# A recurrence's product on VectorE instead of GpSimd, with new rules for the list that orders the engines: a two-layer attention and LSTM kernel on one core

## The chip, the core and the metric

The kernel runs on one core of one Trainium2 chip. The metric is the device time of one execution in microseconds, the median of the runs of a measurement. TensorE (PE in the profile; PEld are its weight loads), VectorE (DVE), ScalarE (ACT), GpSimd (POOL) and SyncE (SP, whose queue issues the DMAs) each work through their own instructions in order and wait for each other by semaphores.

## The reference

Everything is float32. The input `x` is 8 images of 56 x 56 positions with 256 channels. Cut to what matters:

```python
# layer 0: attention between regions of 8 x 8 positions, 49 regions, 8 heads
x = x + conv_attn(group_norm(x))        # each region: its 4 best regions by pooled q.k; 256 keys;
                                        # softmax over the 32 largest of the 256 scores; depthwise 3x3 on v
# layer 1, on t = x as 8 x 3136 tokens
t = t + window_attn(layer_norm(t))      # 7 neighbours
t = t + lstm(layer_norm(t))

def step(carry, xs):                    # 3136 steps, one after the other, 8 images at once, 256 wide
    h, c = carry
    i_t = sigmoid(xi_t + h @ V_i); f_t = sigmoid(xf_t + h @ V_f)   # f_t is computed, but not used
    g_t = tanh(xg_t + h @ V_c);    o_t = sigmoid(xo_t + h @ V_o)
    c_new = h * c + i_t * g_t           # the product h*c of this document
    h_new = o_t * tanh(c_new)
    return (h_new, c_new), h_new
```

The output has the shape of `x`.

## The kernel before

**Two kinds of work.** The recurrence (`recurrence`, one block of 16 tokens, `step(t)` for each token) is one chain of 3136 steps. All the rest, called background here, is layer 0 and the window attention: 56 units of one row of regions of one image (`units`), each with 7 calls of `region`, and the stages `queries_and_lepe`, `project` and `window_attention` of the neighbouring units spread between them. The first row of all images must be through before token 3 can start; the recurrence of one row of regions then goes beside the background of the next; and the last row of tokens (from `APART` = 2685 on) has no background left beside it.

**One step.** `sums_of` adds h times the gates' weights to the input terms that `place_terms` has put into the PSUM bank `r_sum` (24 matmuls of 64 columns, 48 instructions in the trace). ScalarE takes the tanh (`r_th`). VectorE transposes it in blocks of 32 x 32 into the gates' places of a buffer `r_cell`, of which there are two, for even and odd steps. One VectorE scan (`r_c`) then makes the new cell state: `r_cell` holds the gates and, in every third element of one part, the product h*c of the step before. ScalarE takes tanh of half of it (`r_tc`), and VectorE makes h (`r_hs`, from the output gate and that tanh). From token 2685 on, the output gate has sums, a tanh and a transpose of its own (`r_th2`, `r_tr2`).

The product h*c in the version before: ScalarE halves the cell state right after `r_tc` (`r_half`), GpSimd multiplies it with h into the other `r_cell` (line 308 like all of them, since a recorder makes every instruction), and a no-operation of VectorE (`seen_by`) waits for GpSimd's semaphore before the scan of the next step reads it.

**VectorE's background.** A region's 4 x 4 rounds of top-8 (`top`, MAX8) and replacement (`left`, MATCH_REPLACE8) on 128 x 256 scores are most of it. GpSimd's long operations are the subtraction `pe` - `left` (128 x 256) for each of 1568 score tiles, and additions of the same width on `gs`, `v`, `x` and `sum`.

**The list.** `_Plan` records every operation with a duration: `held`, the time it keeps its engine, and `late`, the time to its result, from `_time` or from `nc.timed` and `nc.together`. `run` then goes through time by these durations and takes for each free engine the first ready operation by rank (the chain's first), as long as it would not delay the next chain operation of its engine beyond a slack. What it takes, in that order, is the program's order on each engine; the semaphores follow from the data. `HOP` is the time from one engine to another, `SLACK` and, for VectorE, 1.5 times the time left, say how late an operation may make the chain. Operations with two SBUF operands (`op.pair`) are never listed on VectorE and GpSimd at the same time (`locked`), and long ones of GpSimd must start within three chain operations after h. Where TensorE would be idle for more than `FILL` = 220 ns, the list puts in a matmul whose result nobody reads (`fill`, tile `spare`).

Of the kernel before, what the change touches and what calls it, by code (L numbers as in the profile page):

```python
# [19 lines left out]
P = 128  # L20
# [20 lines left out]
TB = 16  # L41
XB = 8
# [15 lines left out]
HOP = 70  # L58
FAR = 10**12
FILL = 220  # L60
LONG = 400
CLEAR = 250
# [41 lines left out]
def _time(engine, name, view, reads, args, kw):  # L104

    n = max([_count(v) for v in [view] + reads])
    if engine == "SP":
        return 650, 2400 + 9 * n // 4
    if engine == "PE":
        held = 160 if name == "transpose" else 5 * _count(view) // 3 + 50  # L110
        return held, held + 140
    if engine == "POOL":
        t = 180 + 15 * n // 7
        return (1050, 1050) if ALU.pow in args else (t, t)
    if engine == "ACT":
        if kw.get("accum_out") is not None:
            t = 5 * n // 7 + 195
            return t + 90, t + 180
        t = n + 10
        if view.buf.banks:  # L120
            return t + 70, t + 120
        if not any(v.buf.banks for v in reads):
            t += 50
        if isinstance(kw.get("bias"), _View):
            return t + 80, t + 170
        return t, t + 90
    held = 25 * n // 24 + 60
    if name == "reciprocal":
        return 20 * n // 3 + 60, 20 * n // 3 + 150
    if name == "transpose":  # L130
        return held + 40, held + 120
    if name == "tensor_tensor_scan":
        return 2 * n + 80, 2 * n + 170
    if name == "match_replace":
        return held + 65, held + 150
    if name == "scalar_tensor_tensor":
        return held + 20, held + 100
    return held, held + 90
# [72 lines left out]
class _Op:  # L211
    __slots__ = (
        "engine", "trace", "held", "late", "rank", "chain", "before", "open", "due", "start",
        "takes", "pair", "made", "closes", "behind",
# [25 lines left out]
class _Plan:  # L240
# [79 lines left out]
    def seen_by(self, engine, op, view):  # L320


        def trace():
            made = engine.engine.engine_nop()
            self.tc.add_manual_dep(
                made.ins, op.made[0].ins.name,
                mybir.DependencyInfo(mybir.DependencyClass.Sync, mybir.DependencyReason.DATA),
                reason="seen before it is read",
            )

        self.add(engine.name, [trace], [view], [], 10, 10)
        return self.ops[-1]

    def add(self, engine, traces, reads, writes, held, late):
        op = _Op()
        op.engine, op.trace, op.held, op.late = engine, traces, held, late
        op.rank, op.chain = self.mode
        op.rank = (op.rank, len(self.ops))
        op.before, op.takes, op.start = {}, [], None
        op.closes, op.behind = False, None  # L340
        op.pair = engine in ("DVE", "POOL") and sum(
            not v.buf.banks and _count(v) > 8 for v in reads
        ) > 1
        self.ops.append(op)
        for views, write in ((reads, False), (writes, True)):
            for v in views:
                self._depend(op, v, write)
                if v.buf.pool is not None:
                    if not v.buf.users:
                        op.takes.append(v.buf)  # L350
                    if not v.buf.users or v.buf.users[-1] is not op:
                        v.buf.users.append(op)
# [19 lines left out]
    def _edge(self, a, b, whole):  # L372

        gap = a.late + HOP if a.engine != b.engine else a.late + 30 if whole else a.held
        a.before[b] = max(gap, a.before.get(b, 0))


    def run(self, tc, fill):
# [52 lines left out]
        filled = tied = 0  # L431
        locked = {"DVE": 0, "POOL": 0}
        since, closed = 0, None
        while len(done) < len(ops) + filled:
            moved = False
            for e in engines:
# [8 lines left out]
                until = due + (SLACK[e] if e != 'DVE' else max(20, 1.5 * (due - now)))  # L445
                for i, (rank, op) in enumerate(ready[e]):
                    if not op.chain and now + op.held > until:
                        continue
# [9 lines left out]
                    op.start = now  # L458
                    free[e] = now + op.held
# [4 lines left out]
                    heappush(events, now + op.late + HOP)  # L464
# [4 lines left out]
                    for b, gap in op.before.items():  # L469
                        b.due = max(b.due, now + gap)  # L470
                        b.open -= 1
                        if not b.open:
                            opened(b)
                    if op.chain:
                        at += 1
                        since += 1
                        if op.closes:
                            since, closed = 0, op
                    elif e == "POOL" and op.rank[0] == 0:
                        tied += 1  # L480
                    moved = True
                    break
            if not moved and free["PE"] <= now:

                due = min([expected("PE")] + [op[0] for op in later["PE"][:1]])
                if FILL < due - now < FAR // 2:
                    op = _Op()
                    op.trace, op.start = [fill], now
                    filled += 1
                    done.append(op)  # L490
                    free["PE"] = now + FILL
                    heappush(events, free["PE"])
                    moved = True
# [6 lines left out]
        self.length = now  # L500
        with tc.manual_schedule():
            for op in done:
                for t in op.trace:
                    t()

# [24 lines left out]
def _layers(ctx: ExitStack, tc, a, out):  # L530
# [129 lines left out]
    def fill():  # L660
        raw.tensor.matmul(  # L661
            spare[:32, :P], ident[:, :32], ident, start=True, stop=True, skip_group_check=True
# [15 lines left out]
    state = {"seen": None, "h": hss[1][:, :, TB - 1].as_of(hss[1][:, :, TB - 1, LAST:])}  # L678
# [135 lines left out]
    def queries_and_lepe(b, unit, im, row):  # L814
# [81 lines left out]
        def convolve(m):  # L896
            pl = bank()
            for dx in range(3):
                with nc.together(100 * L, 100 * L + 200):
# [22 lines left out]
    def region(qi, unit, im, row):  # L922
# [35 lines left out]
        for pair in range(groups // 2):  # L958
            both = ps_sc.tile([P, 2, 512], F32, name="sc")
            with nc.rank(0.5), nc.together(540, 740):  # L960
# [52 lines left out]
        for k in range(2):  # L1013
            with nc.together(280, 480):
# [11 lines left out]
        with nc.together(350, 550):  # L1026
# [310 lines left out]

    def recurrence(blk):
# [12 lines left out]
        def step(t):  # L1351
# [5 lines left out]
            cell, after = cells[at % 2], cells[(at + 1) % 2]  # L1357
# [5 lines left out]
            if at < APART:  # L1363
                with nc.rank(0, chain=True):
                    sums_of(bank_of(at)[:, now], h, (0, 1, 2), (680, 855))
# [3 lines left out]
                    nc.vector.transpose(gates, blocks(th))  # L1369
            else:  # L1370
# [19 lines left out]
            with nc.rank(0, chain=True):  # L1390
# [11 lines left out]
                if state["seen"]:  # L1402
                    nc._edge(state["seen"], nc.ops[-2], False)
# [5 lines left out]
            half = rwork.tile([P, 2, nb], F32, name="r_half")  # L1409
            nc.scalar.activation(half, c[:, :, :, 2], AF.Copy, scale=0.5)  # L1410
            hc = after[:, CELL + 2 : 2 * CELL + 2].rearrange("p (k b e) -> p k b e", b=nb, e=3)
            nc.gpsimd.tensor_tensor(hc[:, :, :, 2], hn, half, ALU.mult)
            with nc.rank(-1):
                state["seen"] = nc.seen_by(nc.vector, nc.ops[-1], hc[:, :, :, 2])
# [82 lines left out]
    for s in after(len(units) - 1):  # L1497
        s()
    made["tokens"] = SHIFTED
# [70 lines left out]
```

## Time and profile before

| | |
|---|---|
| three runs | 9196.0, 9199.82, 9213.82 us; median 9199.82 |
| the profiled execution | 9180.4 us, span 9178.5 us, granted TensorE clock 0.993 |
| first h of the recurrence starts at | 1340.4 us |
| last h starts at | 9173.2 us |
| busy: PE, DVE, ACT, POOL | 8792.1, 7559.4, 5939.4, 3221.5 us |
| of PE, the fill matmuls on `spare` | 14904 instructions, 2072.2 us |
| instructions | 500794 |

A busy time is the time in which the engine has at least one instruction under way. A duration is from an instruction's start to its end; on VectorE and TensorE the next one can start before that end. Almost all instructions have line 308 in common, where the recorder calls the engine, so they are told apart by their tiles (`out<-in`).

### The profile page before, as it was taken

The numbers are of one execution on the slowest core, as the hardware profiler recorded it, in microseconds if no ns is written. First come the engines' busy times: TensorE is split into PE (matmuls) and PEld (weight loads), VectorE is DVE, ScalarE is ACT, GpSimd is POOL, SyncE is SP. The second block draws the span as 40 slices with busy tenths as digits, with TensorE's granted clock in tenths as the row PEclk, the third lists the DMA queues.
The fourth block names the chain that finished last, engine by engine and source line by source line (L and its number), as shares of the span: only waits on it lengthen the run. The fifth ranks groups of instructions, "written<-read, shape, count | busy, mean of one in ns | idle before, by whom it ended". The sixth has DMA issues, their size and how long they took to land.

```text
span 9178.5 us, 500794 instructions
## 1 busy us (share of the span) xinstructions
PE 8792.1 (96%) x203918; PEld 6037.0 (66%) x203918; DVE 7559.4 (82%) x32392; ACT 5939.4 (65%) x23551; POOL 3221.5 (35%) x7747
## 2 busy tenths in 40 slices
PE   7999999999999999999999999999999999999999
PEld 4555556666666666666666666666666666688888
DVE  5776799999999899999899999899999999734443
ACT  4665667776666677676676676677766766534444
POOL 1232344444343343343344443434434444311111
PEclk9999999999999999999999999999999999999999
DMA  6545433333332333333333333233333232210000
GB/s 198 155 129 163 111 106 82 93 92 80 93 91 78 91 84 90 89 85 91 88 82 92 91 82 90 78 93 88 83 92 89 80 90 78 60 28 23 23 24 21
DMA packets 1071271, 798.40 MB, mean 87 GB/s; under 512 B 402366, under 2 KB 1001524, under 8 KB 1068964
## 3 DMA queue, kind: packets, MB, share of 16 engines
q1 hardware_dynamic: 1068964, 766.36, 30.8%
q8 instruction: 1604, 26.28, 1.2%
q14 instruction: 703, 5.76, 0.2%
HBM read 527.08 MB, written 238.88 MB: 83 GB/s over the span
## 4 chain that ended last, share of the span: by engine, by line
PE 52%; DVE 25%; ACT 6%; issue 2%; DMA 1%; SPq 0%; POOL 0%; ACTq 0%; DVEq 0%; POOLq 0%
PE r_sum L308 19%; PE mm L308 15%; PE spare L661 12%; DVE left L308 8%; DVE top L308 6%; DVE r_c L308 3%; PE pt_av L308 3%; PE sc L308 3%; DVE r_cell L308 2%; DVE r_hs L308 2%; ACT pe L308 1%; ACT r_th L308 1%; ACT xln L308 1%; DVE st L308 1%; ACT r_sum L308 1%
## 5 line engine op out<-in xcount | busy, mean ns | idle before, releaser
L308 PE MATMUL r_sum<-r_v,r_hs 128*16 128x64 f32 (+2 forms) x150528 | 2758.0, 220 | 160.4 <-DVE r_hs L308 107.1
L308 PEld LDWEIGHTS r_sum<-r_v,r_hs 128*8 128x8 f32 (+2 forms) x150528 | 2224.2, 96 | 907.8 <-DVE r_hs L308 802.6
L308 POOL TENSOR_TENSOR r_cell<-r_hs,r_half 128x16 f32<-128x16 f32 x3136 | 706.7, 225 | 4012.7 <-DVE r_hs L308 3192.8
L661 PE MATMUL spare<-ident 128*32 128x128 f32 x14904 | 2072.2, 276 | 6.2 <-issue 4.5
L308 DVE MATCH_REPLACE8 left<-top,left 128x256 f32<-128x256 f32 x4704 | 1903.3, 408 | 0.0
L308 DVE MAX8 top<-left 128x8 f32<-128x256 f32 x4704 | 1848.2, 413 | 1.8 <-POOL r_cell L308 0.3
L308 ACT ACTIVATE r_th<-r_sum 128x64 f32<-128x64 f32 x3587 | 802.3, 224 | 1559.4 <-PE r_sum L308 1507.1
L661 PEld LDWEIGHTS spare<-ident 128*32 128x32 f32 x14904 | 1474.8, 110 | 309.6 <-issue 263.4
L308 DVE STREAM_TRANSPOSE r_cell<-r_th 128x64 f32<-128x64 f32 x3136 | 812.8, 259 | 882.5 <-ACT r_th L308 842.2
L308 POOL TENSOR_TENSOR pe<-pe,left 128x256 f32<-128x256 f32 x1568 | 1136.2, 729 | 821.5 <-ACT left L308 397.9
L308 ACT ACTIVATE r_tc<-r_c 128x16 f32<-128x16 f32 x3136 | 696.9, 222 | 717.4 <-DVE r_c L308 696.0
L308 DVE TENSOR_TENSOR_SCAN r_c<-r_cell 128x48 f32<-128x48 f32 x3136 | 910.8, 290 | 86.9
L308 ACT ACTIVATE pe<-sc,nmax 128x256 f32<-128x256 f32 x1568 | 710.9, 470 | 185.5 <-DVE left L308 105.3
L308 ACT ACTIVATE left<-left,nmax 128x256 f32<-128x256 f32 x1568 | 773.8, 502 | 13.8 <-DVE left L308 7.8
L308 PE MATMUL pt_av<-ident,pe 128*128 128x128 f32 x3136 | 691.2, 289 | 49.4 <-ACT pts L308 19.4
L308 PE MATMUL mm<-wu,xlT 128*112 128x256 f32 (+3 forms) x1856 | 732.6, 512 | 2.6 <-ACT xlT L308 1.7
L308 DVE MAX8 top<-sc 128x8 f32<-128x256 f32 x1568 | 620.4, 416 | 80.8 <-PE sc L308 80.4
L308 ACT ACTIVATE r_half<-r_c 128x16 f32<-128x16 f32 x3136 | 655.3, 209 | 0.0
L308 DVE SCALAR_TENSOR_TENSOR r_hs<-r_cell,r_tc 128x16 f32<-128x16 f32 x2685 | 545.4, 203 | 124.5 <-ACT r_tc L308 103.4
L308 DVE MATCH_REPLACE8 left<-top,sc 128x256 f32<-128x256 f32 x1568 | 641.2, 412 | 0.7 <-issue 0.6
L308 ACT COPY pts<-pt_av 128x256 f32<-128x256 f32 x1568 | 574.8, 367 | 97.6 <-PE pt_av L308 89.5
L308 PEld LDWEIGHTS pt_av<-ident,pe 128*128 128x128 f32 x3136 | 375.3, 143 | 349.2 <-issue 190.0
(131 smaller groups left out, 12151.6 us busy)
## 6 DMA issues: line engine op xcount, KB each, us to landing
kg<-kd SPq DMA_DIRECT2D x1568, 64.0 KB
vg<-vd SPq DMA_DIRECT2D x1568, 64.0 KB
vshift<-lines SPq DMA_DIRECT2D x336, 232.0 KB
xgd<-gs SPq DMA_DIRECT2D x224, 336.0 KB
r_gin<-xgd SPq DMA_DIRECT2D x1568, 48.0 KB
xchunk<-xt SPq DMA_DIRECT2D x112, 448.0 KB
lines<-v SPq DMA_DIRECT2D x112, 290.0 KB
xn<-xh SPq DMA_DIRECT2D x56, 560.0 KB
```

The lines of the kernel that those rows point to most:

```text
L308: made[:] = [method(*[v.real() if isinstance(v, _View) else v for v in args], **{k: v.real() if isinstance(v, _View) else v for k, v in kw ...
L661: raw.tensor.matmul(spare[:32, :P], ident[:, :32], ident, start=True, stop=True, skip_group_check=True)
```

## The change

Five things change together.

- **The product h\*c** is one VectorE instruction, `keep_state`: (h * 0.5) * c into the `r_cell` of the step. While there is background (up to token 2684) it is a part of the chain, listed behind the transpose of the same step's gates and ahead of the scan. From then on it is listed as soon as h is there. ScalarE's `r_half`, GpSimd's product and VectorE's no-operation are gone.
- **GpSimd's long operations with two SBUF operands** wait by a semaphore for the last h that was listed before them (`behind`), beside what they wait for anyway.
- **Loads of input terms** bring 16 tokens (`XB`) instead of 8, into two buffers of twice the size.
- **The list's durations**: TensorE's are shorter (`transpose` 110 instead of 160, matmuls 42n/25 + 4 instead of 5n/3 + 50, and so on), without what a change of the output's height costs; that is held apart as `SWITCH` = 94 ns between operations with outputs of 32, 64 and 128 rows. An operation of another height than 32 must leave that much time before the chain's next sums. Fills can have 32 or 128 rows.
- **The list's reserves**: data that goes from one engine to another for a background operation of rank 0.5 or more is listed as arriving later by `EASE`. VectorE's allowance for delaying the chain is 0.2 or 2.0 times the time left instead of 1.5, by whether its background is ahead of an even spread over the steps that have background (`yields`).

```diff
-XB = 8
+XB = 16
 HOP = 70
+SWITCH = 94
+EASE = {"PE": 120, "ACT": 60, "POOL": 250, "DVE": 120, "SP": 0}
+AHEAD = 0.02
-FILL = 220
+FILL = 218
-CLEAR = 250
+CLEAR = 200
@@ _time
-        held = 160 if name == "transpose" else 5 * _count(view) // 3 + 50
-        return held, held + 140
+        held = 110 if name == "transpose" else 42 * _count(view) // 25 + 4
+        return held, held + 190
@@ _Plan._edge
+        if a.engine != b.engine and not b.chain and b.rank[0] >= 0.5:
+            gap += EASE[b.engine]
@@ _Plan.run
+        def yields():
+            ahead = spent - begun - (at / beside + AHEAD) * (work - begun)
+            return 0.2 if ahead > 0 else 2.0
+        def lag_of(form2):
+            return max(0, ended + SWITCH - now) if form2 != form else 0
...
-                until = due + (SLACK[e] if e != 'DVE' else max(20, 1.5 * (due - now)))
+                until = due + (SLACK[e] if e != "DVE" else max(20, yields() * (due - now)))
...
+                    if e == "PE":
+                        lag = lag_of(op.form)
+                        if not op.chain and op.form != 32 and now + lag + op.held + SWITCH > until:
+                            continue
-                    if not op.chain and now + op.held > until:
+                    if not op.chain and now + lag + op.held > until:
...
-                if FILL < due - now < FAR // 2:
+                whole = form != 32 and due - now > 2 * FILL + SWITCH
+                lag = lag_of(P if whole else 32)
+                if FILL + lag < due - now < FAR // 2:
...
+                if getattr(op, "behind", None):
+                    self.tc.add_manual_dep(op.made[0].ins, op.behind.made[0].ins.name, ...)
@@ _layers
+    def keep_state(cell):
+        h, c = state["past"]
+        hc = cell[:, CELL + 2 : 2 * CELL + 2].rearrange("p (k b e) -> p k b e", b=nb, e=3)
+        nc.vector.scalar_tensor_tensor(hc[:, :, :, 2], h, 0.5, c, ALU.mult, ALU.mult)
+        nc.timed(92, 150)
...
-                    sums_of(bank_of(at)[:, now], h, (0, 1, 2), (680, 855))
+                    sums_of(bank_of(at)[:, now], h, (0, 1, 2), (671, 855))
...
                     nc.vector.transpose(gates, blocks(th))
+                    turned = nc.ops[-1]
+                    if state["past"]:
+                        keep_state(cell)
+                        turned.before[nc.ops[-1]] = turned.held
...
-            half = rwork.tile([P, 2, nb], F32, name="r_half")
-            nc.scalar.activation(half, c[:, :, :, 2], AF.Copy, scale=0.5)
-            hc = after[:, CELL + 2 : 2 * CELL + 2].rearrange("p (k b e) -> p k b e", b=nb, e=3)
-            nc.gpsimd.tensor_tensor(hc[:, :, :, 2], hn, half, ALU.mult)
-            with nc.rank(-1):
-                state["seen"] = nc.seen_by(nc.vector, nc.ops[-1], hc[:, :, :, 2])
+            state["past"] = hn, c[:, :, :, 2]
+            if APART <= at + 1 < SHIFTED:
+                with nc.rank(-1):
+                    keep_state(cells[(at + 1) % 2])
```

The order of the programs: all background instructions are the same in kind and number. VectorE has 3135 products more and 3136 no-operations fewer, ScalarE 3136 halvings and GpSimd 3136 products fewer, SP 784 loads instead of 1568; fills go from 7452 to 8393, 2138 of them with 128 rows (each is two instructions in the trace).

## Prediction

> **What bounds the kernel now.** I read the page first, then the answer for the tiles of one recurrence step, then windows cut where the stages change, then the timeline of single steps. The page says that TensorE is busy nearly all the time, but this is no bound by itself: 2072 us of it are the fill matmuls on `spare`. The chain that ended last changes engine all the way.
>
> ```profile
> span 9178.5 us, 500794 instructions
> PE 8792.1 (96%) x203918; PEld 6037.0 (66%) x203918; DVE 7559.4 (82%) x32392; ACT 5939.4 (65%) x23551; POOL 3221.5 (35%) x7747
> PE 52%; DVE 25%; ACT 6%; issue 2%; DMA 1%; SPq 0%; POOL 0%; ACTq 0%; DVEq 0%; POOLq 0%
> ```
>
> The answer for the tile `r_cell` and that for `r_hs` give each chain operation's shortest, median and longest time in ns, and its first and last start:
>
> ```profile
> L308 DVE TENSOR_TENSOR_SCAN r_c<-r_cell x3136: 212/258/814, 1339.9 to 9172.7; 128x48 f32<-128x48 f32 x196
> L308 POOL TENSOR_TENSOR r_cell<-r_hs,r_half x3136: 218/225/235, 1340.8 to 9173.5; 128x16 f32<-128x16 f32 x196
> L308 DVE SCALAR_TENSOR_TENSOR r_hs<-r_cell,r_tc x2685: 142/175/696, 1340.4 to 8215.8; 128x16 f32<-128x16 f32 x192
> L308 DVE SCALAR_TENSOR_TENSOR r_hs<-r_tr,r_tc x451: 174/176/177, 8217.9 to 9173.2; 128x16 f32<-128x16 f32 x151
> ```
>
> So there are three stages: 1340 us before the first step; 2684 step intervals in 8215.8 - 1340.4 = 6875 us, 2.562 us each; and 450 in the tail, 955 us, 2.123 each. The windows for the tile `r_c` split the second stage further (DVE busy, with its count, then ACT):
>
> ```profile
> 1340.00:8000.00 6660.00, 778.64 (x2590) 870.93 (x5180) 1.00 0.32 87
> 8000.00:8216.00 216.00, 25.35 (x95) 32.01 (x190) 1.00 0.12 30
> ```
>
> With background work beside it a step takes 6660/2590 = 2.571 us; the last 95 steps, when that work has run out, take 216/95 = 2.27. Both have the same chain. The second stage is thus bound by the recurrence at 2.27 plus 0.30 us per step that the background costs it. I read where the 0.30 sits by taking every step of the trace apart (mean of steps 100 to 2500 against the quiet steps): h itself 204 against 176 ns, h to TensorE's start 121 against 56, the sums 894 against 859, to the tanh 97 against 67, tanh to transpose 89 against 32, the scan 301 against 268, scan to the second tanh 75 against 34, that to h 49 against 32. By cause: TensorE late 100 ns, ScalarE late 71, VectorE full 74, and the two VectorE operations with two SBUF operands stretched by 61. The stretch is a GpSimd operation in flight:
>
> ```profile
> 2574.02 0.72 POOL L308 TENSOR_TENSOR pe<-pe,left 128x256 f32<-128x256 f32 x1 [1.04 <-ACT left L308]
> 2574.09 0.68 DVE L308 SCALAR_TENSOR_TENSOR r_hs<-r_cell,r_tc 128x16 f32<-128x16 f32 x1
> ```
>
> Here h starts 0.07 us behind a 0.72 us subtract of GpSimd and takes 0.68 us where its median is 0.175; both end together.
>
> **The change, part by part.** All sums are against the profiled run (9180.4 us, span 9178.5); the median of the three runs, 9199.8, is 0.2% above it, and I shift the result by that difference. About 0.2%, 18 us, is what a measurement here can tell from no change.
>
> *h\*c on VectorE.* GpSimd's 3136 products (225 ns) and ScalarE's 3136 halvings (655 us busy) go, and VectorE's no-operation that waited for GpSimd. In steps 1 to 2684 the new operation stands between the transpose and the scan, and the scan reads what it writes. This timeline of VectorE shows the place with an operation that happened to stand there:
>
> ```profile
> 1341.99 0.27 DVE L308 STREAM_TRANSPOSE r_cell<-r_th 128x64 f32<-128x64 f32 x1
> 1342.15 0.14 DVE L308 RECIPROCAL inv<-tot 128x4 f32<-128x4 f32 x1
> 1342.29 0.26 DVE L308 TENSOR_TENSOR_SCAN r_c<-r_cell 128x48 f32<-128x48 f32 x1
> ```
>
> A small operation can start about 0.169 us after the transpose's start (median of such pairs), and the scan starts 0.298 after it, 34 ns behind the transpose's end. The product has the form of `r_hs`, 175 ns, and the scan must wait for its end: 0.169 + 0.175 + 0.034 = 0.378 instead of 0.298, so 80 ns on the chain of every step, 2684 x 0.080 = +215 us. Bounds: 0 if the scan waited only for the product's issue (an `r_hs` lets the next one start after 0.09), and +0.209 (561 us) if the product could start only at the transpose's end. I take 0.080, because the reciprocal's row starts before the transpose ends.
>
> The Trainium skill's page "VectorE: DVE Perf Modes", section "The DRAIN you can't avoid", speaks against this edit: the next operation does not start until the pipeline is empty. The rows above show a start 0.11 us before the transpose's recorded end, so I do not use it; by it the product would cost the 561 us and the kernel would be slower by 5%.
>
> In the tail the product follows h at once, while VectorE idles about 1 us for the tanh, so it costs nothing; were that cover gone, 450 x 0.09 = 40 us.
>
> *GpSimd's long operations behind h.* The product also was what held GpSimd's queue to h once a step. Now the long ones (456 to 729 ns, about one per step) wait for the preceding h by semaphore and are listed so that they should end before the next pair. Behind such a wait stand the rest of GpSimd's queue (`nmax`, `gs`, `sum`), and for them wait ScalarE's exponentials and TensorE's transposes of `pe`. The gain at stake is the stretch: the scan's mean of 290 against its median 258 over 3136, 100 us, and h's 203 against 175 over 2685, 75 us: 175 us, all on the chain. GpSimd starts 0.28 us earlier after h, since its own product is gone, so most should clear: -140 (from 0 to -175).
>
> *TensorE's durations and the reserve.* In the trace a late hand-over (over 60 ns) has TensorE's contents plus about 100 ns for each change between 128-row, 64-row and 32-row outputs (two changes: 300 ns over the contents; three: 400; four: 470 to 550). The old list reserved nothing for that, and its transposes were 160 where 110 is enough. The new one reserves 94. Of the 100 ns by which TensorE is late, 2590 x 0.100 = 259 us, I take half, -130 (0 to -220), as operations may still be listed up to the slack and late data still blocks the queue in order.
>
> *ScalarE.* Without the halving, and with 80 ns more between the two tanhs, a 0.5 us exponential fits there more often: of 71 ns x 2590 = 184 us I take -50 (0 to -100).
>
> *Background spread.* The order of the program has the last top-8 work at step 2564 before and at step 2630 after, and other VectorE background up to step 2683. The 95 quiet steps turn busy, at some 0.2 us each: +19; the same work over 2684 steps is 3.5% less VectorE load in each, for which I take a tenth of VectorE's 74 ns x 2590 = 192 us: -20 (0 to -60). The last gates now stand wholly between the sums of step 2684 and 2685: 28 matmuls of 13.9 us by their lengths and 19 fills of 0.218, 18 us where an ordinary step has 1.5: +17 (0 to +25).
>
> *Before the first step.* The order holds 129 more fills there (28 us by 0.218) and 38 more top-8 operations on VectorE (13 us by 0.33 to 0.39). TensorE has 1340 - 1192 = 148 us idle there, which hides most fills: +15 (0 to +40).
>
> *16-token loads.* 784 issues of `r_gin` in place of 1568, about 0.43 us of SP's queue each, and a load is due 16 steps ahead rather than 8. Only the stalls on DMAs could gain (1% of the chain, 92 us, few of it `r_gin`): 0 to -30, taken as 0. Fills in all rise from 7452 to 8393; they lie in gaps, and where one is late it is in TensorE's term.
>
> Sum: 215 - 140 - 130 - 50 + 19 - 20 + 17 + 15 = -74. The run shown becomes 9106, the median 9200 - 74 = 9126; I say 9130. The second stage then runs at about 2.53 us per step.
>
> **The rivals.**
> - *The product outweighs what it frees (slower).* The product's 80 ns is certain in kind, the 320 us of gains are hopes on hand-overs. If the stretch gives back only 70 and TensorE's late hand-overs only 60, about half of what I took, and ScalarE nothing, the sum is 215 - 130 + 31 = +116: 9316. It decides where less than 246 us, or 92 of the 302 ns per step, comes back. For it: the step already has little free room on VectorE (1.7 us of background against windows of 1.32 + 0.38 us per quiet step), so a delay removed at one hand-over may return as VectorE's at the next.
> - *It cancels.* Gains of about 250: 9200 within 18. This is the decision point itself, so narrow.
> - *The reserve does all that it says.* TensorE's -220, the stretch's -175, ScalarE's -100: 215 - 495 + 31 = -249: 8950. Against it: TensorE's contents with fills and changes come to 2.37 us per step in the new order, by these lengths, so a step could not fall under that; 2.47 is what this case needs.
> - *The long GpSimd operations now meet the product*, a third pair operation per step, and arrive late: the stretch stays at 175 and TensorE's share halves: +215 - 65 - 50 + 31 = +131. I count it with the first rival.
>
> **How the numbers follow.** Forecast (sum between -150 and -18) 0.40; full reserve (below -150) 0.17; cancels 0.11; slower 0.32. Faster is 0.57, same 0.11, slower 0.32. The range goes from the full-reserve case, 8960, to the first rival's 9316 and a little over, 9330; within it lies the forecast's own range of 9050 to 9182.
>
> **What would show it.** Right: the scan's start 0.37 to 0.39 after the transpose's; medians of h and scan unchanged, with means within 10 ns of them; h to TensorE's start under 85 ns on average; second stage 2.50 to 2.55 us per step; no quiet stretch before the tail; tail still 2.12. Wrong: a product that starts only at the transpose's end, a stretch that remains on scan or product, transposes of `pe` waiting for GpSimd ahead of the sums, or a first step later than 1380 us.

## The result, and the profile after

The changed kernel takes 9276.94 us, the median of four runs (9266.14 to 9300.11), against 9204.43 us (9196.0 to 9213.82) for four runs of the kernel before: 1.0087 times, 95% interval 1.0075 to 1.0099. It is slower, where 9130 and faster was forecast; the range of 8960 to 9330 holds it. Its profiled execution took 9266.14 us, against 9180.4 before.

The head of its page, and three of its groups (busy us and mean ns, then the idle time just before and its releaser):

```profile
span 9264.4 us, 494939 instructions
PE 8911.2 (96%) x205800; PEld 6337.3 (68%) x205800; DVE 7759.3 (84%) x35527; ACT 5604.7 (60%) x20415; POOL 2561.9 (28%) x4611
PE 60%; DVE 25%; ACT 6%; issue 2%; DMA 2%; SPq 0%; POOL 0%; ACTq 0%; POOLq 0%; DVEq 0%
...
L311 POOL TENSOR_TENSOR pe<-pe,left 128x256 f32<-128x256 f32 x1568 | 1147.5, 733 | 2948.7 <-DVE r_hs L311 1939.3
...
L311 DVE TENSOR_TENSOR_SCAN r_c<-r_cell 128x48 f32<-128x48 f32 x3136 | 897.3, 286 | 87.0
...
L311 DVE SCALAR_TENSOR_TENSOR r_cell<-r_hs,r_c 128x16 f32<-128x16 f32 x3135 | 564.4, 180 | 14.7
```

ScalarE and GpSimd do less, as the change says. The subtract now waits for h (1939 us of GpSimd's idle time). TensorE's transposes of `pe` behind it do not suffer: their waits for GpSimd's `pe` sum to 28 us, and were 69 before. The third group is the product. Its rows, and those of the scan and of h, in the answers for the tiles `r_cell` and `r_hs` (min, median, max in ns):

```profile
L311 DVE TENSOR_TENSOR_SCAN r_c<-r_cell x3136: 212/258/745, 1308.3 to 9258.7; 128x48 f32<-128x48 f32 x196
L311 DVE SCALAR_TENSOR_TENSOR r_cell<-r_hs,r_c x3135: 127/143/734, 1310.6 to 9257.4; 128x16 f32<-128x16 f32 x196
L311 DVE SCALAR_TENSOR_TENSOR r_hs<-r_cell,r_tc x2685: 147/175/730, 1309.0 to 8282.0; 128x16 f32<-128x16 f32 x192
L311 DVE SCALAR_TENSOR_TENSOR r_hs<-r_tr,r_tc x451: 174/176/305, 8303.4 to 9259.3; 128x16 f32<-128x16 f32 x151
```

The stages are cut at the first and last starts of h. The first step starts 31 us earlier (1309.0, was 1340.4). The 2684 steps of the second stage take 8282.0 - 1309.0 = 6973 us, 2.598 each (was 2.562): +98. Then the hand-over to the tail takes 21.4 us (was 2.1): +19. The tail takes 955.8 (was 955.3). Together +86, the difference of the spans.

The windows for the tile `r_c` (DVE busy with its count, then ACT) show what became of the quiet steps before the tail:

```profile
1310.00:8000.00 6690.00, 1220.16 (x5142) 574.12 (x2571) 1.00 0.32 84
8000.00:8282.00 282.00, 51.28 (x226) 25.23 (x113) 1.00 0.22 56
```

These count the scan and the product, two per step: 6690/2571 = 2.602 us per step with the background beside it, and 282/113 = 2.50 in the last stretch.

By the same taking apart of steps 100 to 2500 as in the prediction, a step grew by 30 ns (2573 to 2603). Smaller: h 204 to 184, h to TensorE 121 to 113, the sums 894 to 889, to the tanh 97 to 83, tanh to transpose 89 to 84, the scan 301 to 295. Larger: from the transpose's end to the scan 38 to 123, where the product now stands, and scan to the second tanh 75 to 79. The place of the product in an undisturbed step is 47 ns (the median from the transpose's end to the scan goes from 34 to 81). Most of the rest of the 85 is the product's own stretch beside GpSimd:

```profile
2601.30 2.11 POOL L311 TENSOR_TENSOR gs<-gs,bu 112x256 f32<-112x256 f32 x3
...
2601.60 0.27 DVE L311 STREAM_TRANSPOSE r_cell<-r_th 128x64 f32<-128x64 f32 x1
...
2601.77 0.31 DVE L311 SCALAR_TENSOR_TENSOR r_cell<-r_hs,r_c 128x16 f32<-128x16 f32 x1
...
2602.11 0.72 DVE L311 TENSOR_TENSOR_SCAN r_c<-r_cell 128x48 f32<-128x48 f32 x1
...
2603.14 0.30 DVE L311 SCALAR_TENSOR_TENSOR r_hs<-r_cell,r_tc 128x16 f32<-128x16 f32 x1
```

In this timeline of one step three additions on `gs` run in a row, and product (0.31 for 0.143), scan (0.72 for 0.258) and h (0.30 for 0.175) each wait for the end of one of them. Summed over the steps between 1340 and 8216 us, the time above 0.262 us of a scan and above 0.18 of an h or a product, where it was more than 20 ns longer (called the stretch below), was 192 us before (scan 112, h 80; 127 of it behind the subtract `pe`), and is 215 us after: scan 98, h 28, product 88. Behind the subtract alone it is now below 1 us, and nearly all lies behind `gs` + `bu`, `x` + `bo` and `v` + `bv`.

Why those: `op.pair`, by which the list locks an operation against VectorE's and gives it the semaphore behind h, counts only operands that the recorder wraps. `bu`, `bo` and `bv` (`bv1` in the code) are plain constant tiles. So these additions, 972 in the records of the second stage, count as operations with one operand, and are neither locked nor made to wait. What is said of the lock and the semaphore ahead of the prediction holds for the subtract and the addition on `sum` alone. Before, GpSimd's own product held its whole queue to h once per step. Now the subtract starts 170 ns (median) after h's end, in place of 795, but the additions on `gs` at 1516 instead of 776, where the next step's transpose and scan are due.

### The profile page after: what moved, and what is told of

Its sections match the earlier page's. It is cut to its first block, busy times and chain, and to the rows that moved or that the text cites. A ratio compares the mean times of both kernels' runs of the same rounds, so it can differ in the third digit from the quotient of the medians.

```text
span 9264.4 us, 494939 instructions
## 1 busy us (share of the span) xinstructions
PE 8911.2 (96%) x205800; PEld 6337.3 (68%) x205800; DVE 7759.3 (84%) x35527; ACT 5604.7 (60%) x20415; POOL 2561.9 (28%) x4611
## 4 chain that ended last, share of the span: by engine, by line
PE 60%; DVE 25%; ACT 6%; issue 2%; DMA 2%; SPq 0%; POOL 0%; ACTq 0%; POOLq 0%; DVEq 0%
PE r_sum L311 19%; PE mm L311 19%; PE spare L693 14%; DVE left L311 8%; DVE top L311 6%; PE pt_av L311 5%; DVE r_cell L311 4%; DVE r_c L311 3%; PE sc L311 3%; DVE r_hs L311 2%; ACT pe L311 1%; ACT r_th L311 1%; DMA xn<-xh 1%; ACT xln L311 1%; ACT left L311 1%
## 5 line engine op out<-in xcount | busy, mean ns | idle before, releaser
L311 PE MATMUL r_sum<-r_v,r_hs 128*8 128x64 f32 (+2 forms) x150528 | 2749.2, 220 | 201.2 <-DVE r_hs L311 170.0
L693 PE MATMUL spare<-ident 128*32 128x128 f32 (+1 forms) x16786 | 2380.3, 277 | 14.3 <-issue 12.7
L693 PEld LDWEIGHTS spare<-ident 128*32 128x32 f32 (+1 forms) x16786 | 1795.6, 131 | 277.6 <-issue 140.8
L311 PE MATMUL mm<-wu,xlT 128*112 128x512 f32 (+2 forms) x1856 | 739.0, 512 | 2.6 <-ACT xlT L311 2.4
L311 DVE SCALAR_TENSOR_TENSOR r_hs<-r_cell,r_tc 128x16 f32<-128x16 f32 x2685 | 494.3, 184 | 138.9 <-ACT r_tc L311 125.8
L311 ACT ACTIVATE et<-top,nmax 128x32 f32<-128x32 f32 x1568 | 497.0, 318 | 138.7 <-DVE top L311 122.9
L311 DVE SCALAR_TENSOR_TENSOR r_cell<-r_hs,r_c 128x16 f32<-128x16 f32 x3135 | 564.4, 180 | 14.7
```

The lines of the kernel that those rows point to most:

```text
L311: made[:] = [method(*[v.real() if isinstance(v, _View) else v for v in args], **{k: v.real() if isinstance(v, _View) else v for k, v in kw ...
L693: raw.tensor.matmul(spare[:n, :P], ident[:, :n], ident, start=True, stop=True, skip_group_check=True)
```

## The experiments

All times are medians, and each ratio is to runs of the kernel before on the same chip. That kernel took 9187 to 9192 us on the chips of these runs and 9204 on that of the result, so two versions are compared by their ratios, and the difference is given in us of 9200. Unless it is said otherwise, the edit is on the changed kernel. "Border" means the hand-over to a new row of regions, every 448 steps.

**1. The constants made visible to the list.**

```diff
+    bo, bv1, bu = nc.fixed(bo, (QB, C)), nc.fixed(bv1, (KB, C)), nc.fixed(bu, (QB, GATES * C))
     cells = [nc.fixed(t, (P, WIDE)) for t in cells]
```

> The changed kernel, with the constants bo, bv1 and bu known to the list, so that GpSimd's additions on gs, x and v count as two-operand operations (kept apart from VectorE's pairs, behind h by semaphore). Theory A (the time went to these additions: 215 us of stretch on product, scan and h, all but 1 us of it behind them, since only GpSimd's own product had gated them): the stretch falls under 40 us, step 2.53 us in the second stage, about 9277 - 180 = 9095 us. Theory B (the product's 47 ns per step on the chain is the cost, the stretch is covered and comes back as another wait): 9240 to 9277. Theory C (the new list rules make the loss): as B, 9277 within 20.

Measured: 9262.3 us, 1.0083 [1.0066, 1.0100]. The answers for `r_cell` and `r_hs`:

```profile
L311 DVE TENSOR_TENSOR_SCAN r_c<-r_cell x3136: 214/257/672, 1311.3 to 9251.6; 128x48 f32<-128x48 f32 x196
L311 DVE SCALAR_TENSOR_TENSOR r_cell<-r_hs,r_c x3135: 128/142/694, 1313.6 to 9250.3; 128x16 f32<-128x16 f32 x196
L311 DVE SCALAR_TENSOR_TENSOR r_hs<-r_cell,r_tc x2685: 147/175/182, 1312.0 to 8251.1; 128x16 f32<-128x16 f32 x192
```

The longest h falls from 730 to 182 ns, and the whole stretch from 215 to 5 us. So the cause of the stretch is shown. A step of up to 5 us takes 2.523 us on average instead of 2.593, 189 us over the stage. But the ratio hardly moves (1.0083 after 1.0087, each within the other's interval): steps 445, 893, 1341, 1789 and 2237 now take 34 to 38 us each and the hand-over at 2685 takes 45. What the steps over 5 us take beyond 2.5 us each sums to 210 us, where the changed kernel has 32. The timeline at the first border:

```profile
2431.70 0.17 DVE L311 SCALAR_TENSOR_TENSOR r_hs<-r_cell,r_tc 128x16 f32<-128x16 f32 x1
...
2445.20 1.41 POOL L311 TENSOR_TENSOR gs<-gs,bu 112x256 f32<-112x256 f32 x2 [3.49 <-ACT gs L311]
...
2463.90 0.47 ACT L311 COPY r_sum<-r_gin 128x128 f32<-128x128 f32 x2
...
2464.23 0.86 PE L311 MATMUL r_sum<-r_v,r_hs 128*8 128x64 f32 x48 [0.36 <-ACT r_sum L311]
...
2466.37 0.17 DVE L311 SCALAR_TENSOR_TENSOR r_hs<-r_cell,r_tc 128x16 f32<-128x16 f32 x1
```

The sums wait for the copy of new input terms (`r_gin`) into PSUM, and those come out of the additions on `gs` of the last unit of the row. The first of them starts 13.5 us into the gap, and not behind h: GpSimd waits there for ScalarE's `gs`, so the work ahead of the additions is late already.

**2. Is it GpSimd's capacity, one place per step?** The bias of the gates goes to TensorE as a third matmul, which takes the additions on `gs` away; the other two constants are visible to the list.

```diff
-                        start=(k == 0), stop=(k == 1),
+                        start=(k == 0), stop=False,
...
+                nc.tensor.matmul(pg[:q, : g - f], ident[:q, :q], bu[:q, f:g], start=False, stop=True)
...
-                nc.gpsimd.tensor_tensor(gs[:, f : f + C], gs[:, f : f + C], bu[:q, f : f + C], ALU.add)
```

> The run with the constants known to the list (9262), and the gates' bias no longer added by GpSimd: TensorE adds it into the same PSUM sums, as a third matmul with the identity as weights. Theory D (GpSimd has one free place per step for a 0.73 us operation, between h and the next pair; there were 1.03 such operations per step, so they either collide or the recurrence starves at the row borders): without the 576 additions it is 0.82 per step, the 35 us waits at steps 445, 893, 1341, 1789 and 2237 go, the stretch stays under 15 us, ordinary steps stay near 2.52: about 9262 - 180 = 9080, below both kernels. Rival E (TensorE becomes the bound: 1.3 us more matmul for each of 192 blocks, 93 ns per step, not covered by fills): steps of 2.60, 9280 or more.

Measured: 9325.35 us, 1.0145 [1.0128, 1.0162]. GpSimd has 0.80 operations of over 0.4 us per step in the second stage instead of 1.03 (experiment 1), yet the borders still take 31 to 35 us, and the hand-over at 2685 takes 65. The same border in its timeline:

```profile
2463.26 0.17 DVE L311 SCALAR_TENSOR_TENSOR r_hs<-r_cell,r_tc 128x16 f32<-128x16 f32 x1
...
2495.34 0.48 ACT L311 COPY r_sum<-r_gin 128x128 f32<-128x128 f32 x2
2495.67 0.69 PEld L311 LDWEIGHTS r_sum<-r_v,r_hs 128*8 128x8 f32 x48 [0.18 <-ACT r_sum L311]
```

It is the same wait without any addition on `gs`. The capacity theory falls: what is late is the last unit of the row as a whole. What makes the list put it late was not found. The rival's 9280 and more came true, but not its reason: steps of up to 5 us take 2.529 us, not 2.60.

**3. Is it VectorE's allowance?** Experiment 1 with `AHEAD` 0.06 in place of 0.02.

```diff
-AHEAD = 0.02
+AHEAD = 0.06
```

> The run with the constants known to the list (9262), with VectorE's background kept 6% of its work ahead of an even spread instead of 2% (AHEAD 0.06). If the waits of 35 us at the row borders come from background that is spread too evenly and so ends late, they go, and ordinary steps stay near 2.52 to 2.54: 9100 to 9150, below both kernels. If GpSimd's places for long operations bound it after all: 9262 within 40.

Measured: 9262.92 us, 1.0081 [1.0064, 1.0098]; the borders still take 35 to 38 us. This is no lever either.

**4. The product right behind h, with experiment 1 and with experiment 2.** The product is taken out of the chain and listed like that of the tail.

```diff
-                    turned = nc.ops[-1]
-                    if state["past"]:
-                        keep_state(cell)
-                        turned.before[nc.ops[-1]] = turned.held
...
-            if APART <= at + 1 < SHIFTED:
+            if at + 1 < SHIFTED:
```

> The run with the constants known to the list (9262), gates' bias still on GpSimd, and the product as soon as h is there. Theory D: GpSimd's places still bound it: ordinary steps a little shorter, waits at the row borders still there or longer: 9200 to 9262. If the waits at the borders came from VectorE's pacing or the product's place instead, they would shrink by more than half: 9100.

Measured with experiment 1: 9227.62 us, 1.0039 [1.0024, 1.0053]. The time is in the range of theory D, but the waits at the borders, on which it stood, are gone; instead 40 steps of 5 to 7 us are spread over the stage (128 us together beyond 2.5 us each), and the others take 2.545. The mean from tanh to transpose rises to 206 ns: VectorE's queue is now what comes late.

> The same as the run with the bias on TensorE, and the product listed as soon as h is there on all steps, so that it is no longer between transpose and scan. Theory D: 47 ns per step leave the chain and VectorE's full stretch after h takes 90 ns: a net 20 ns per step, 50 us below that run: about 9030. Rival F (VectorE is the bound there): the same as that run or up to 60 us above it.

Measured with experiment 2: 9601.07 us, 1.0448 [1.0431, 1.0466]: borders of 29 to 73 us, 39 more steps of 5 to 7 us and 2.597 in the rest, with 191 ns from tanh to transpose. Neither theory has that. Why the same edit gains 40 us on one list and loses 276 on the other isn't settled.

**5. The product alone, on the list of before.** The kernel before with `keep_state` in the place that the change gives it; no semaphore, no new rule.

```diff
+                    if state["past"]:
+                        keep_state(cell)
...
-            half = rwork.tile([P, 2, nb], F32, name="r_half")
-            nc.scalar.activation(half, c[:, :, :, 2], AF.Copy, scale=0.5)
...
-            nc.gpsimd.tensor_tensor(hc[:, :, :, 2], hn, half, ALU.mult)
-            with nc.rank(-1):
-                state["seen"] = nc.seen_by(nc.vector, nc.ops[-1], hc[:, :, :, 2])
+            state["past"] = hn, c[:, :, :, 2]
```

> The kernel before, with only the product moved to VectorE: old list, no semaphore for GpSimd's long operations. Theory A: 126 us for the product, and the stretch grows over the 192 us of before, as nothing holds GpSimd's queue to h, on the subtractions too: +50 to +150; 9380 to 9480. Theory B: 9204 + 126 = 9330 with a stretch like before. Theory C (the product is harmless, the list is to blame): 9204 within 30.

Measured: 9626.0 us, 1.0475 [1.0458, 1.0493], beyond even theory A's 9480. The answers for `r_cell` and `r_hs`:

```profile
L308 DVE TENSOR_TENSOR_SCAN r_c<-r_cell x3136: 215/257/2083, 1347.8 to 9628.3; 128x48 f32<-128x48 f32 x196
L308 DVE SCALAR_TENSOR_TENSOR r_cell<-r_hs,r_c x3135: 128/143/2052, 1350.1 to 9627.0; 128x16 f32<-128x16 f32 x196
L308 DVE SCALAR_TENSOR_TENSOR r_hs<-r_cell,r_tc x2685: 144/176/1122, 1348.4 to 8669.8; 128x16 f32<-128x16 f32 x192
```

The medians are those of the changed kernel, but single operations wait up to 2 us behind GpSimd, which nothing holds to h any more. The stretch is 432 us, 240 more than before; with the 126 of the product's place that is 366 of the 438 us lost. The other parts of the change then win back about 350 us (1.0475 to 1.0087): beside the product they are worth much, and the sum of the prediction had the right parts paying for each other. How much of the 350 is the semaphore and how much the list's order was not tried by itself.

**6. The list's rules without the product.** The product goes back to GpSimd, with ScalarE's halving and VectorE's no-operation, and `XB` to 8.

```diff
-XB = 16
+XB = 8
...
-                    if state["past"]:
-                        keep_state(cell)
...
-            state["past"] = hn, c[:, :, :, 2]
+            half = rwork.tile([P, 2, nb], F32, name="r_half")
+            nc.scalar.activation(half, c[:, :, :, 2], AF.Copy, scale=0.5)
...
+            nc.gpsimd.tensor_tensor(hc[:, :, :, 2], hn, half, ALU.mult)
```

> The changed kernel, with the product back on GpSimd (halving on ScalarE, VectorE's no-operation) and 8-token loads, which leaves room for the halved state: the list rules alone against the kernel before. Theory A: the product gates the additions again, their stretch is back near 65 us, and 126 us of product go from the chain: 9277 - 126 - 150 = about 9000. Theory B: the 126 us alone: 9150. Theory C: still over 9204.

Measured: 9293.6 us, 1.0113 [1.0096, 1.0130]. The stretch is 85 us, but the scan now often waits for GpSimd's product (from the transpose's end 111 ns on average, 218 in the 90th percentile, against 38 on average before), and steps over 5 us, the borders with 16 to 33 us and the hand-over with 42 among them, take 151 us beyond 2.5 us each. Theory C, over 9204, came true. On the new list with 8-token loads, then, the product is better on VectorE: 9188 (next experiment) against 9294. On the old list, without the semaphore, it is worse by 438.

**7. Undoing the loads.** `XB` = 8; then, apart from that, each 16-token load issued as two DMAs of 8 tokens with the list left as it is.

```diff
-XB = 16
+XB = 8
```

> The changed kernel with 8-token loads: 16-token loads undone alone. If they did nothing, 9277 within 20; if their relief of SP's queue was worth something, 9290 to 9320.

Measured: 9188.35 us, 0.9999 [0.9990, 1.0009]: 81 us less than the changed kernel by the ratios, from one number that was priced at 0.

```diff
-                nc.sync.dma_start(gins[t // XB % 2][...], xg[n][...])
+                with nc.together(*_time("SP", "", gins[0][:, :m], [], (), {})):
+                    for f in range(0, m, 8):
+                        z = min(f + 8, m)
+                        nc.sync.dma_start(gins[t // XB % 2][..., f:z], xg[n][...])
```

> The changed kernel with its own list, but every 16-token load issued as two of 8 tokens, listed in the same place with the same duration: all other engines keep the changed kernel's order. Theory G (the 89 us that came back with 8-token loads came from another list, not from the transfers): 9277 within 20. Theory H (the larger transfers themselves hold the recurrence up): 9190 to 9220.

Measured: 9285.2 us, 1.0111 [1.0095, 1.0128]. So smaller transfers alone win nothing back; the list that the larger block leads to costs the 81 us. With `XB` = 8 the step of the second stage is 2.568 us instead of 2.598, 80 us over the stage, of which the stretch is 172 - 215 = -43 us and scan to the second tanh 66 against 79 ns, -35 us. The rows of h, for `XB` = 8:

```profile
L311 DVE SCALAR_TENSOR_TENSOR r_hs<-r_cell,r_tc x2685: 142/175/742, 1307.2 to 8199.8; 128x16 f32<-128x16 f32 x192
L311 DVE SCALAR_TENSOR_TENSOR r_hs<-r_tr,r_tc x451: 174/175/311, 8218.3 to 9174.6; 128x16 f32<-128x16 f32 x151
```

Its second stage still takes 8199.8 - 1307.2 = 6893 us, 18 more than before; the earlier first step pays for that and for the hand-over of 18.5 us.

**8. How far a meaningless change of the list moves the time.** `FILL` 218 to 219, 1 ns of a planned duration, on the changed kernel and on `XB` = 8.

```diff
-FILL = 218
+FILL = 219
```

> The changed kernel, with the length that the list takes for a fill at 219 ns instead of 218; nothing else. Theory G: the list falls out otherwise, and the time moves by some tens of us, to either side: 9180 to 9300, not 9277 within 10. Theory H or any theory by which the five parts have fixed prices: 9277 within 15.

> The changed kernel with 8-token loads and one number of the list altered that means nothing by itself (FILL 218 to 219, 1 ns of a planned duration). Theory A (the 8-token list is better for a reason that a trivial change of the list does not move): 9188 us within 20, 9168 to 9208. Rival B (the gain of the 8-token list was a lucky draw among lists): it comes back by half or more, 9230 to 9285 us.

Measured: 9259.36 us with 16-token loads, 1.0077 [1.0060, 1.0094], 9 us under the changed kernel, which is within the intervals; 9188.32 with 8-token loads, 0.9998 [0.9988, 1.0007], the same as without it. The row of h in the second:

```profile
L311 DVE SCALAR_TENSOR_TENSOR r_hs<-r_cell,r_tc x2685: 140/174/841, 1297.5 to 8201.3; 128x16 f32<-128x16 f32 x192
```

Even its stages move by about 10 us each (the first step by 10, the second stage 6904 for 6893) and cancel. The 81 us of the loads are well outside what these two draws show.

**9. TensorE's earlier durations, without the reserve,** with 16-token and with 8-token loads.

```diff
-SWITCH = 94
+SWITCH = 0
...
-        held = 110 if name == "transpose" else 42 * _count(view) // 25 + 4
-        return held, held + 190
+        held = 160 if name == "transpose" else 5 * _count(view) // 3 + 50
+        return held, held + 140
...
-                whole = form != 32 and due - now > 2 * FILL + SWITCH
+                whole = False
```

(and `FILL` = 220 and the earlier planned times of the sums and of TensorE's bundles.)

> The changed kernel with TensorE's old durations in the list and no reserve for a change of height, fills of 32 rows and 220 ns: that part undone. If the new durations and the reserve bring what I forecast (130 us): 9340 to 9420. If they bring what the traces' lateness of TensorE says (13 ns per step, 34 us): 9300 to 9330. By theory G the list's own scatter of tens of us lies on top.

> The changed kernel with two of its parts undone: TensorE's earlier durations in the list with no reserve at hand-overs and no whole hand-over at the end, and 8-token loads; the product on VectorE and the semaphores behind h stay. Alone, the durations undone gave 9223 us (54 under the changed kernel) and the 8-token loads 9188 (89 under it). Theory A (each of the two parts costs by its own mechanism, so what undoing them gains adds): 9277 - 54 - 89 = 9134 us, 9115 to 9155, below both kernels. Rival B (both gains are one: any other list than the changed kernel's falls back to the same ordinary place of GpSimd's additions, so they do not add): 9170 to 9225 us. Under A VectorE's stretch beside GpSimd falls below 160 us; under B it stays between 160 and 200 us, as in each of the two alone.

Measured: 9223.35 us with 16-token loads, 1.0037 [1.0023, 1.0051], where both theories had a loss against the changed kernel, and 9234.56 with 8-token loads, 1.0048 [1.0031, 1.0065]. The row of h in the second:

```profile
L311 DVE SCALAR_TENSOR_TENSOR r_hs<-r_cell,r_tc x2685: 147/174/735, 1332.1 to 8270.0; 128x16 f32<-128x16 f32 x192
```

| | 8-token loads | 16-token loads |
|---|---|---|
| new TensorE durations | 9188 (0.9999) | 9277 (1.0087) |
| earlier TensorE durations | 9235 (1.0048) | 9223 (1.0037) |

Theory A of the last run falls: the two parts don't add, and the combination misses even the rival's range by 10 us, though its stretch of 166 us lies where the rival put it. With 8-token loads the new durations gain 45 us (54 between the profiled executions): the first step starts 25 us earlier (1307 for 1332), the second stage takes 45 us less (6893 for 6938), and the long hand-over at 2685 (2.2 to 18.5 us) takes some of it back. With 16-token loads they lose 46. Neither edit has a price of its own here. In three of the four corners the stretch is 164 to 172 us, and 213 to 215 in the changed kernel, with `FILL` = 219, and in the split loads, which share the list of the changed kernel. Why the list puts GpSimd's unordered additions worse in that corner stays open.

**10. The constants made visible in the kernel before.** The edit of experiment 1 there.

> The kernel before, with the constants known to the list as in the run on the changed kernel; product still on GpSimd. Theory A: the additions' share of the stretch, 65 of 192 us, goes: about 9150. Theory B: no change, 9204 within 20.

Measured: 9203.75 us, 1.0014 [1.0004, 1.0023]. The stretch falls from 192 to 167 us, and h to the sums rises from 121 to 140 ns. The old list loses a little more than it gains.

No version was faster than the kernel before by more than can be measured; the changed kernel with 8-token loads equals it.

## Why the prediction was wrong

The sum of the prediction, term by term, with what the profiled runs show in its place (us):

| step | predicted | measured |
|---|---|---|
| product's place on the chain | +215 | +126 |
| stretch beside GpSimd | -140 | +23 |
| TensorE late | -130 | -34 |
| ScalarE late | -50 | -26 |
| spread of the background | +19 - 20 | +16 - 16 |
| last gates before the tail | +17 | +19 |
| before the first step | +15 | -31 |
| loads, by their transfers | 0 | 0 |
| sum | -74 | +77 (spans: +86) |

The measured column takes the differences of the means above: 47 ns x 2684 for the product; 215 - 192 for the stretch; (8 + 5) ns x 2590 for TensorE, (14 - 4) for ScalarE and (5 + 1) for VectorE; and 95 x 0.16 us for the quiet steps, the last 95 ahead of the tail, which went from 2.28 to 2.49 us, 0.047 of it the product.

**The step that failed is the stretch.** The prediction took 175 us of stretch from the trace, showed a subtract as its cause, and let the new semaphore clear 140 of it. The subtract's 127 us did go. But a third of the old stretch lay behind additions with a constant operand, and the prediction did not ask which of the long operations the rule would catch. The answer was in the code (`op.pair` counts recorded views) and in the order of the program. What had held those additions was GpSimd's own product, which the change took away (with it back, the additions cost 83 us in experiment 6; without it, 168 in experiment 7, on 8-token loads both); the prediction named this ("the product also was what held GpSimd's queue to h") and then gave the whole duty to the semaphore. The fourth rival came nearest: the stretch stays and the product is a third operation that meets it. It said 175 us and +131 in all, but did not tell the additions from the subtract. The failure does not hang on the unlucky list of the 16-token loads: with 8-token loads the stretch is 172 us, 20 less than before, where 140 less was forecast. Experiment 1 shows that with the additions ordered as well the stretch goes, further than forecast, and that the cost comes back at the borders, which no rival had. Of the signs that the prediction named, those against it came true: a stretch that remained on scan and product, h to TensorE at 113 ns and not under 85, and 2.598 us per step, not 2.50 to 2.55.

**TensorE's term was four times too large.** The lateness went from 100 to 87 ns per step. Undoing the reserve raises h to TensorE and the sums to 135 and 900 ns (experiment 9, 16-token loads; with 8-token loads it raises them likewise, by 26 and 7 ns), so the mechanism is there; yet with 16-token loads that kernel is faster, because VectorE's lateness before the transpose (57 for 84 ns) and the stretch (164 for 215 us) fall. This is the caution of the first rival: a delay taken from one hand-over returns at another.

**The product's place** was right in kind and too dear. The starting point of 0.169 us after the transpose's start holds, but the product takes 143 ns there and not the 175 of `r_hs`: 0.169 + 0.143 + 0.034 = 0.346, and the trace shows a median of 0.344. The reciprocal in the fence of the prediction, 0.14 in the same place, was the nearer row. Right behind h the same product does take 175 (experiment 4). The 126 us were measured against the 561 that the rule on the pipeline's drain of the Trainium skill's page "VectorE: DVE Perf Modes" (section "The DRAIN you can't avoid") would have given. That section sends the reader on to "Two Vector instructions with no wait between them", by which an instruction that isn't held starts earlier, and that is the case the rows show. (The slowdown of 5% that the prediction set beside the 561 us is not its own sum: with 561 in place of 215 the sum is +272 us, 3%.)

**Right were** the tail at no cost (955.8 for 955.3), the hand-over at 2685 (+19 for +17), the loss of the quiet steps and VectorE's gain, this last perhaps by luck: its lateness before the transpose, 89 to 84 ns, also moves from 84 to 57 by another list alone (experiment 9). **Before the first step** the sign was wrong: 129 more fills and 38 more top-8 operations were counted there, and the step came 31 us earlier. With the earlier durations in the list it comes at 1328 to 1332 (experiment 9), with the new ones and the same work on TensorE at 1297 to 1316 (experiments 1, 4, 6, 7 and 8), so most of the gain is TensorE's shorter planned durations, for which the prediction had looked only inside the second stage.

**The loads** cost nothing as transfers, as said; but an edit that changes the input of a list also draws another list, and that was priced at 0 where two cases here show a gain of 10 and a loss of 81 us.

## What to carry to other kernels

Before a rule is credited with removing a stall, list by operand which instructions stand behind that stall, and look up for each whether the rule reaches it; and when an instruction is removed, ask what its wait was holding in order. Where a program decides the order of instructions, the price of an edit is not its own: draw a second, meaningless change of the list to learn its scatter (1 and 9 us here), and cross two edits before giving either its number (here the 16-token loads cost 81 us or gain 10, and the durations gain 45 or cost 46). When ordinary steps get faster, look at the rare long ones too: experiment 1 gained 189 us on the ordinary steps and gave 178 back, nearly all of it in six.

## What the runs showed of the hardware

A VectorE operation with two SBUF operands that starts beside a long GpSimd one waits for about its end. In the changed kernel, beside the additions on `gs`, `v` and `x` with more than 200 ns left, the time above the typical is the remaining time less about 145 ns for the scan and h, and less about 102 for the products that were held (means): 597 ns left behind `gs` cost the scan 453, 605 left behind `v` cost h 461, and 476 left behind `gs` cost the product 374 over its 143. Not every product was held: 32 of 288 took their usual time, and each of these had started within 45 ns of the addition's start. One of them, with the scan behind it that was held instead (the second of the two additions starts at about 1744.94):

```profile
1744.27 1.45 POOL L311 TENSOR_TENSOR gs<-gs,bu 112x256 f32<-112x256 f32 x2
...
1744.98 0.14 DVE L311 SCALAR_TENSOR_TENSOR r_cell<-r_hs,r_c 128x16 f32<-128x16 f32 x1
...
1745.16 0.67 DVE L311 TENSOR_TENSOR_SCAN r_c<-r_cell 128x48 f32<-128x48 f32 x1
```

And not every long GpSimd operation holds VectorE:

```profile
1799.37 1.04 POOL L311 TENSOR_TENSOR rs<-rs,mhalf 112x4 f32<-112x4 f32 x1
...
1799.64 0.26 DVE L311 TENSOR_TENSOR_SCAN r_c<-r_cell 128x48 f32<-128x48 f32 x1
```

This power of four elements per partition lasts 1.04 us, and the scan that starts 0.77 us before its end takes its usual 0.26; over all such cases in the changed kernel, 31 scans with 742 ns left and 64 h with 670 left (means), the mean excess is -2 and -1 ns. The Trainium skill's page "SBUF — State Buffer", section "Who interferes with whom", calls the port that the two engines share an exclusive lock. The waits behind the additions agree with it. The same page, section "Terms", has the lock held for the full instruction, and this row differs: the power, which moves few elements, did not block for as long as it lasts. GpSimd was busy with it all the same, since its next instruction never starts less than 0.99 us after it.
